# Out-projection of an attention block by seven quarter products per pair of heads, on normalised probabilities

## The chip, the cores and the metric

The kernel runs on one core of a Trainium2 chip. The metric is the device time of one execution in microseconds; the median of three runs before the change is 1045.25 us (1043.97 to 1045.48). Times of single instructions come from one profiled execution.

The engines are TensorE (PE; its weight loads are listed as PEld), VectorE (DVE), ScalarE (ACT), GpSimd (POOL) and SyncE (SP), which here only issues DMAs. Each works through its own instructions in order. [...]

## What is computed

The reference is a transformer block with adaptive LayerNorm, all in fp32: batch 2, 1024 tokens, width 256, 16 heads of 128.

```python
h = layernorm(x) * (1 + ca) + sa
q, k, v = h @ Wq + bq, h @ Wk + bk, h @ Wv + bv      # 16 heads of 128; rotary on q and k
attn = softmax(causal(q @ k.T * 128 ** -0.5))        # per head, 1024 x 1024
x = x + ga * ((attn @ v) joined over heads @ Wo + bo)
h = layernorm(x) * (1 + cb) + sb
x = x + gb * down(silu(gate(h)) * up(h))             # 704 hidden, int32 weights with scales
```

`sa, ca, ga, sb, cb, gb` come from a small product of `silu(c)` with `wmod`.

## The kernel before

Tokens lie on 128 partitions in 8 tiles (`NT`) or, turned, in two halves of 512 columns (`NB` blocks). The unit of work is one head of one batch: 32 units, `units[n] = (b, g, h)`, two heads `h` to a pair `g`, eight pairs to a batch. Everything sits in one hand-written order, `with tc.manual_schedule()` (L1008): what the program emits is the order of each engine's queue, and there is no planner.

The main loop (L1064) runs over units and within a unit over eight rows `i`, one per tile of 128 queries. A row does this:

- `shared_out` (L1004) emits one tile of the out-projection of an earlier unit, 13 rows behind.
- `score` (L601): TensorE computes `ps`, 128 queries against (i + 1) x 128 keys, into one of two score buffers; one DVE instruction adds the mask in place and gives the negated row maximum `nmax`.
- `turned` (L643) of the row before: DVE turns 32 x 32 blocks of the probabilities into `t32`; after each fourth row SP issues 16 DMAs that move the blocks across partitions into `pT` (one block of queries). `t32` has four slots of equal size for the four rows of a block.
- `expo` (L628): ACT computes the exponential of the row and, in the same pass, its sum `dens`.
- `set_step` (L464): the products of q, k and v of the coming units. From the second pair on, a 1024 x 256 by 256 x 256 projection is already made of seven products of quarters with sums of quarters, with adds on DVE, ACT and POOL and sums of weights on POOL (`weight_sums`).
- rotary embedding (`rotary_sums`, L583): two ACT copies and three POOL operations for each half of q or k, at rows set by `TURNS`.
- `values` (L663): `po` = v-transposed times `pT`, for the unit before: block 0 in row 0 (four matmuls), block 1 in rows 6 and 7 (eight). One PSUM bank holds `po`; ACT copies it to `outs`.
- `extras` (L912): the weight fold, LayerNorm pieces of the next stage, weight loads of the FFN, and the like.

The probabilities are not normalised. `project_out` (L708) multiplies a tile of `outs` with the head's part of Wo (128 x 256) into the single bank `py`, and one DVE instruction adds it to x, times the reciprocal of the row sum:

```python
nc.vector.scalar_tensor_tensor(
    x[b][:, t, :], py[:, :D], rdens[u][:, t : t + 1], x[b][:, t, :], ALU.mult, ALU.add
)
```

So each pair has 16 such matmuls of 256 columns, each with weights of its own (a tile of `outs`), and 16 updates of x. `fold_out` (L382) multiplies Wo with the gate `ga` on POOL, in row 2 of a pair's first unit, and for batch 0 it also gathers what the bias of v gives through Wo. `bias_row` (L397) turns that into a row with one matmul in unit 16, and `add_bias` (L406) adds it to x by 16 POOL operations.

The last unit runs the first products of the FFN of batch 0 in its rows. After the loop come the rest of the FFN products, the out-projection tiles still owed, and the FFN of batch 1.

Of the kernel before, what the change touches and what calls it, by code (L numbers as in the profile page):

```python
# [37 lines left out]
def adaln_block(ctx: ExitStack, tc: tile.TileContext, a, cos_d, sin_d, out):  # L38
# [74 lines left out]
    bvacc = const.tile([P, D], F32, name="bvacc")  # L113
# [100 lines left out]
    opool = pool("attnT", 2)  # L214
# [99 lines left out]
    def ffn_weight_load(n):  # L314
        if n == "gate":
            t = fpool.tile([P, KC * 2 * HID], I32, tag="f", name="raw")
            at = 0
            for m, w in (("gate", FULL), ("up", FULL), ("last", P)):
                raws[m] = t[:, at : at + KC * w].rearrange("p (k h) -> p k h", k=KC)
                at += KC * w  # L320
        nc.scalar.dma_start(raws[n], a[f"wq_{n}"])
# [6 lines left out]
    def ffn_down_load():  # L328

        for c, (pool_, tag, bufs) in (  # L330
# [3 lines left out]
            nc.scalar.dma_start(t, a["wq_down"][:, c : c + 2, :])  # L334
        sbc["down"] = small.tile([P, D], F32, tag="bw", bufs=1, name="s_down")
        nc.scalar.dma_start(sbc["down"], a["scales"][:, 2 * HID :].to_broadcast([P, D]))
# [38 lines left out]
    def load_out(b, g):  # L375
        t = wpool.tile([P, HG, D], F32, tag="wo", name=f"wo_{b}{g}")
        nc.sync.dma_start(
            t, a["L0_attn_Wo"][g]
        )
        weights[b, g]["o"] = t  # L380

    def fold_out(b, g):  # L382
        t = weights[b, g]["o"]
        if b == 0:

            for h in range(HG):
                c = R_BV + g * HG + h
                bw = small.tile([P, D], F32, tag="bw", bufs=1, name=f"bw_{g}{h}")
                nc.gpsimd.tensor_scalar(bw, t[:, h, :], cols[:, c : c + 1], None, ALU.mult)
                nc.gpsimd.tensor_tensor(bvacc, bvacc, bw, ALU.add)  # L390

        for h in range(HG):
            nc.gpsimd.tensor_tensor(t[:, h, :], t[:, h, :], gate["a", b], ALU.mult)

    gbo = {}

    def bias_row():  # L397

        pb = ps_a.tile([P, 512], F32, tag="a", name="pbias")
        nc.tensor.matmul(pb[:, :D], ones, bvacc, start=True, stop=True)  # L400
        nc.vector.tensor_tensor(bo_bc, pb[:, :D], bo_bc, ALU.add)
        gbo.update({0: bvacc, 1: bo_bc})
        for b in range(B):
            nc.gpsimd.tensor_tensor(gbo[b], gate["a", b], bo_bc, ALU.mult)

    def add_bias(b, t):  # L406
        nc.gpsimd.tensor_tensor(x[b][:, t, :], x[b][:, t, :], gbo[b], ALU.add)

    vs, qks, outs, dens, rdens, probs, pTs = {}, {}, {}, {}, {}, {}, {}
    weights = {}  # L410
# [230 lines left out]
    t32 = [const.tile([P, 4, 4, 4 * (j + 1), 32], F32, name=f"t32_{j}") for j in range(NB)]  # L641

    def turned(u, i):  # L643
# [4 lines left out]
            t32[blk][:, :, j, : i + 1, :].rearrange("p c k b -> p k c b"),  # L648
            p[:, : (i + 1) * P].rearrange("p (k c a) -> p k c a", c=4, a=32),
        )  # L650
        if j < 3:
            return
        pT = ptpool.tile(
            [P, 4, 4, 4 * (blk + 1), 32], F32, tag=f"pT{blk}", name=f"pT_{b}{g}{h}{blk}"
# [8 lines left out]
    def values(u, blk, k0, k1):  # L663
        b, g, h = u
        if blk == 0 and k0 == 0:
            outs[u] = opool.tile([P, S], F32, tag="o", name=f"o_{b}{g}{h}")
        if k0 == 0:
            pos[u, blk] = ps_o.tile([P, 512], F32, tag="o", name=f"po_{b}{g}{h}{blk}")
        po = pos[u, blk]
        last = 4 * blk + 3  # L670
        pT = pTs[u, blk].rearrange("p r i k b -> p i r k b")
        for k in range(k0, k1):
# [4 lines left out]
                pT[:, off:, :, k, :],  # L677
# [3 lines left out]
        if k1 == last + 1:  # L681
            nc.scalar.copy(outs[u][:, ts(blk, QB)], po)  # L682
# [25 lines left out]
    def project_out(u, t, late=False):  # L708

        b, g, h = u  # L710
        if t % 4 == 0:
            nc.vector.reciprocal(rdens[u][:, t : t + 4], dens[u][:, t : t + 4])
        name = f"py_{b}{g}{h}{t}"
        py = lane(name) if late else ps_y.tile([P, 512], F32, tag="y", name=name)
        nc.tensor.matmul(  # L715
# [196 lines left out]
    def extras(n, i):  # L912

        if i == (2 if n else 7) and units[n][2] == 0:
            fold_out(*units[n][:2])
# [336 lines left out]
```

## Time and profile before

| | |
|---|---|
| median of the runs | 1045.25 us |
| profiled execution | 1044.49 us |
| its span on the core | 1042.7 us |
| instructions | 13636 |
| granted TensorE clock | 1.00 |
| DMA traffic | 131.86 MB, mean 126 GB/s |
| scores (L613) / values (L674) / out-projection (L715), share of the chain that ended last | 22% / 23% / 10% |

The page gives for each engine its busy time and share of the span. A line of the groups names the source line, engine, operation, tiles written and read, shape and count; then the busy time of the group and the mean duration of one in ns; then the engine's idle time just before them with what ended it. A line of the timeline begins with start and duration in us, and ends, in brackets, with the idle time before it and its releaser. An fp32 matmul is recorded as two MATMUL instructions, and a record includes the time in which the last columns leave the array, so that neighbours overlap. A few matmul records can be missing.

### The profile page before, as it was taken

How to read it: one execution, taken by the hardware profiler on the slowest of the kernel's cores; microseconds unless marked ns; L12 is line 12 of the kernel's file. 1: busy time of each engine (PE TensorE's matmuls, PEld its weight loads, DVE VectorE, ACT ScalarE, POOL GpSimd, SP SyncE). 2: the span in 40 equal slices, each digit the busy share in tenths (PEclk: the TensorE clock that was granted, in tenths of full speed). 3: DMA queues.
4: the chain of work that ended last, by engine and by line, in shares of the span. 5: the costliest groups of instructions: out<-in, count | busy, mean ns of one | idle time of the engine just before them, and what ended most of it. 6: DMA issues, size and time to landing. Idle time of an engine off the chain costs nothing.

```text
span 1042.7 us, 13636 instructions
## 1 busy us (share of the span) xinstructions
PE 1029.0 (99%) x3766; PEld 623.5 (60%) x3766; DVE 759.5 (73%) x1619; ACT 506.3 (49%) x997; POOL 745.6 (72%) x768
## 2 busy tenths in 40 slices
PE   9999999999999999999999999999999999999998
PEld 5655565656556565656565666656565656555737
DVE  5667877787777777767776767677878866787573
ACT  5654545555545445455555554554635545353230
POOL 4738787979787878998787878787876778831131
PEclk9999999999999999999999999999999999999999
DMA  5365555665554545665555545454555557532101
GB/s 193 82 180 137 150 131 144 165 162 147 132 138 103 137 120 143 154 152 124 124 145 122 134 116 144 111 141 110 148 131 128 141 138 176 130 76 62 45 1 41
DMA packets 67616, 131.86 MB, mean 126 GB/s; under 512 B 19110, under 2 KB 22708, under 8 KB 67540
## 3 DMA queue, kind: packets, MB, share of 16 engines
q1 hardware_dynamic: 65292, 125.65, 49.1%
q10 hardware_dynamic: 2168, 5.20, 1.5%
q8 instruction: 31, 0.51, 0.2%
q14 instruction: 45, 0.37, 0.1%
q0 software_dynamic: 80, 0.13, 0.1%
HBM read 25.52 MB, written 2.10 MB: 26 GB/s over the span
## 4 chain that ended last, share of the span: by engine, by line
PE 89%; DVE 6%; POOL 2%; DMA 1%; issue 1%; ACT 1%; SPq 0%; DVEq 0%; POOLq 0%; ACTq 0%
PE po L674 23%; PE ps L613 22%; PE py L715 10%; PE pv L489 8%; PE pq L493 8%; PE pk L493 7%; PE pgu L766 4%; PE pd L878 2%; PE pq L552 1%; PE pk L552 1%; PE pv L420 1%; PE pd_0w L878 1%; PE pd_1w L878 1%; DVE x L718 1%; DMA cols<-in_biases 1%
## 5 line engine op out<-in xcount | busy, mean ns | idle before, releaser
L633 ACT ACTIVATE p<-ps,nmax 128x128 f32<-128x128 f32 (+7 forms) x256 | 189.7, 741 | 356.3 <-DVE nmax L616 347.7
L613 PE MATMUL ps<-kT,qT 128*128 128x512 f32 (+3 forms) x768 | 289.9, 486 | 1.0 <-POOL kT L592 1.0
L674 PE MATMUL po<-pT,v 128*128 128x512 f32 (+3 forms) x768 | 263.4, 486 | 0.0
L616 DVE CUSTOM_DVE_ANT_0 ps<-ps,mask 128x128 f32<-128x128 f32 (+7 forms) x256 | 195.1, 762 | 77.9 <-PE ps L613 75.8
L674 PEld LDWEIGHTS po<-pT,v 128*128 128x128 f32 x768 | 144.7, 190 | 134.2 <-issue 106.2
L718 DVE SCALAR_TENSOR_TENSOR x<-py,rden,x 128x256 f32<-128x256 f32 x255 | 121.5, 478 | 133.0 <-PE py L715 128.7
L647 DVE STREAM_TRANSPOSE t<-p 128x128 f32<-128x128 f32 (+7 forms) x256 | 198.2, 774 | 7.6 <-ACT p L633 3.6
L613 PEld LDWEIGHTS ps<-kT,qT 128*128 128x128 f32 x768 | 145.7, 190 | 78.8 <-issue 63.6
L715 PE MATMUL py<-wo,o 128*128 128x256 f32 x510 | 153.0, 384 | 6.2 <-DVE x L718 6.2
L715 PEld LDWEIGHTS py<-wo,o 128*128 128x128 f32 x510 | 87.7, 191 | 80.1 <-issue 49.7
L590 POOL TENSOR_TENSOR r_k<-r_k,sin_t 128x512 f32<-128x512 f32 x56 | 71.3, 1273 | 84.6 <-ACT r_k L589 84.5
L590 POOL TENSOR_TENSOR r_q<-r_q,sin_t 128x512 f32<-128x512 f32 x56 | 71.9, 1285 | 27.5 <-ACT r_q L589 25.3
L589 ACT COPY r_q<-qT 64x512 f32<-64x512 f32 x112 | 69.1, 617 | 29.0 <-POOL qT L500 27.3
L592 POOL TENSOR_TENSOR kT<-kT,r_k 128x512 f32<-128x512 f32 x56 | 71.2, 1271 | 4.4
L592 POOL TENSOR_TENSOR qT<-qT,r_q 128x512 f32<-128x512 f32 x56 | 71.0, 1267 | 4.4
L591 POOL TENSOR_TENSOR qT<-qT,cos_t 128x512 f32<-128x512 f32 x56 | 71.3, 1273 | 0.0
L591 POOL TENSOR_TENSOR kT<-kT,cos_t 128x512 f32<-128x512 f32 x56 | 71.2, 1272 | 0.0
L589 ACT COPY r_k<-kT 64x512 f32<-64x512 f32 x112 | 69.1, 617 | 2.2 <-DVE kT L500 0.2
L682 ACT COPY o<-po 128x512 f32<-128x512 f32 x64 | 37.5, 586 | 43.6 <-PE po L674 43.4
L489 PEld LDWEIGHTS pv<-wv,tT 128*128 128x128 f32 x336 | 44.1, 192 | 17.1 <-issue 11.2
L774 POOL TENSOR_TENSOR gsnap<-gsnap,gsnap 128x512 f32<-128x512 f32 x8 | 10.5, 1308 | 56.2 <-DVE gsnap L774 56.2
L633 ACT ACTIVATION_READ_ACCUMULATOR p<-ps,nmax 128x1 f32 x256 | 49.4, 193 | 0.0
(222 smaller groups left out, 1495.4 us busy)
## 6 DMA issues: line engine op xcount, KB each, us to landing
pT<-t SPq DMA_DIRECT2D x512, 128.0 KB, 2.4
pT<-t SPq DMA_DIRECT2D x512, 64.0 KB, 2.0
wq<-in_Wq SPq DMA_DIRECT2D x16, 256.0 KB, 3.1
wk<-in_Wk SPq DMA_DIRECT2D x16, 256.0 KB, 2.9
wv<-in_Wv SPq DMA_DIRECT2D x16, 256.0 KB, 2.8
wo<-in_Wo SPq DMA_DIRECT2D x16, 256.0 KB, 2.9
out<-x SPq DMA_DIRECT2D x15, 128.0 KB, 1.7
x<-in_x ACTq DMA_DIRECT2D x4, 256.0 KB, 3.9
```

The lines of the kernel that those rows point to most:

```text
L493: nc.tensor.matmul(bank, wq, tokens, start=True, stop=True)
L589: nc.scalar.copy(r1[to], q[of])
L590: nc.gpsimd.tensor_tensor(r1, r1, sin_t[:, sl], ALU.mult)
L591: nc.gpsimd.tensor_tensor(q, q, cos_t[:, sl], ALU.mult)
L592: nc.gpsimd.tensor_tensor(q, q, r1, ALU.add)
L613: nc.tensor.matmul(ps[:, c:e], qT[:, ts(i, P)], kT[:, c:e], start=True, stop=True)
L616: nc.vector.tensor_tensor_reduce(ps[:, :L], ps[:, :L], mask[:, NT - 1 - i :, :].rearrange("p t k -> p (t k)"), -SCALE, FLT_MAX, ALU.add, A ...
L633: nc.scalar.activation(p[:, :L], ps[:, :L], AF.Exp, bias=nmax, scale=-1.0, accum_out=dens[u][:, i : i + 1])
L647: nc.vector.transpose(t32[blk][:, :, j, : i + 1, :].rearrange("p c k b -> p k c b"), p[:, : (i + 1) * P].rearrange("p (k c a) -> p k c a", ...
L674: nc.tensor.matmul(po[:, off * P :], vs[b, g][:, k, ts(h, DH)], pT[:, off:, :, k, :], start=(k == 0), stop=(k == last),)
L715: nc.tensor.matmul(py[:, :D], outs[u][:, ts(t, P)], weights[b, g]["o"][:, h, :], start=True, stop=True)
L718: nc.vector.scalar_tensor_tensor(x[b][:, t, :], py[:, :D], rdens[u][:, t : t + 1], x[b][:, t, :], ALU.mult, ALU.add)
```

## The change

For each pair of heads but the last one of batch 1 (`direct`), the out-projection is done by seven quarter products in place of sixteen tile products. The 1024 tokens are halved (`blk`), the pair's 256 rows of Wo are halved by head, and the 256 output columns are halved. `out_product` makes one product of 512 tokens by 128 columns, four matmuls of 128 x 128; left factors are quarters of `outs` or their sums (`out_sum`, four DVE operations per pair), right factors are quarters of Wo or their differences (four POOL operations per pair in `fold_out`). Three products go straight to x (one of them subtracted), four are gathered over the pairs of a batch in `m1`, `m5`, `m6`, `m7`, and after the batch's last pair `out_total` brings those to x by eight operations. `OUTS`, `SUMS` and `TOTALS` give the rows: a pair's products lie in rows 2, 6 and 7 of the second unit after its first head, and 0, 2, 4 and 6 of the next.

Sums over two heads need normalised heads. So each row has, after its exponential, a reciprocal of its one column of `dens` on DVE (`inverse`) and a pass of ACT over the row's probabilities with that column as scale (`divided`), before the turn. The bias of v is added where ACT evacuates `po`; the gathered bias products, the bias matmul and the additions to x go, and `bias_row` now puts the gated output bias into `m1` and `m5`.

The turned probabilities are packed: row j of a block starts at slot `STEP * j`, so that `t32` and `pT` have 13 and 29 slots in place of 16 and 32. `outs` has single buffers per half and head, and memory freed or needed elsewhere moves: the FFN weights are loaded in place, two chunks of the FFN's activations share the `m` buffers. The fold of Wo moves to row 6 of a pair's first unit. The load of the down weights moves from ACT's queue at unit 29, row 7, to SP's queue at unit 30, row 5. The load of Wo comes after that of Wk. At unit 16 the turns of rows 0 and 1 change places. In the last unit row 5 has no FFN products; after the loop come 3 tile products instead of 2 (or 3) in each group, and 7 FFN products instead of 5 in the last call. The totals of batch 1 fall into rows 3 to 7 of the last unit, in part on POOL.

```diff
     def fold_out(b, g):
         t = weights[b, g]["o"]
-        if b == 0:
-            for h in range(HG):
-                c = R_BV + g * HG + h
-                bw = small.tile([P, D], F32, tag="bw", bufs=1, name=f"bw_{g}{h}")
-                nc.gpsimd.tensor_scalar(bw, t[:, h, :], cols[:, c : c + 1], None, ALU.mult)
-                nc.gpsimd.tensor_tensor(bvacc, bvacc, bw, ALU.add)
         for h in range(HG):
             nc.gpsimd.tensor_tensor(t[:, h, :], t[:, h, :], gate["a", b], ALU.mult)
+        if (b, g) == direct:
+            return
+        b11, b12, b21, b22, t1, t2, t4 = wquarters[b, g]
+        for to, x0, x1 in ((t1, b12, b11), (t2, b22, t1), (b12, b22, b12), (t4, t2, b21)):
+            nc.gpsimd.tensor_tensor(to, x0, x1, ALU.subtract)
...
+    STEP = [4 * blk + 3 for blk in range(NB)]
+    SLOTS = [3 * STEP[blk] + 4 * (blk + 1) for blk in range(NB)]
+    def inverse(u, i):
+        nc.vector.reciprocal(rdens[u][:, i : i + 1], dens[u][:, i : i + 1])
+    def divided(u, i):
+        p = probs[u, i][:, : (i + 1) * P]
+        nc.scalar.activation(p, p, AF.Copy, scale=rdens[u][:, i : i + 1])
...
         if k1 == last + 1:
-            nc.scalar.copy(outs[u][:, ts(blk, QB)], po)
+            c = R_BV + g * HG + h
+            nc.scalar.activation(outs[u, blk], po, AF.Identity, bias=cols[:, c : c + 1])
...
+    def out_sum(b, g, n):
+        h0, h1 = ((b, g, h) for h in range(HG))
+        if n == 3:
+            osum[3] = opool.tile([P, QB], F32, tag="oC", name=f"o3_{b}{g}")
+            nc.vector.tensor_tensor(osum[3], outs[h0, 1], outs[h0, 0], ALU.subtract)
+        elif n == 1:
+            osum[1] = outs[h0, 0]
+            nc.vector.tensor_tensor(osum[1], osum[1], outs[h1, 0], ALU.add)
+        elif n == 2:
+            osum[2] = outs[h0, 1]
+            nc.vector.tensor_tensor(osum[2], osum[1], osum[2], ALU.subtract)
+        else:
+            osum[4] = opool.tile([P, QB], F32, tag="oC", name=f"o4_{b}{g}")
+            nc.vector.tensor_tensor(osum[4], outs[h1, 1], osum[2], ALU.subtract)
...
+    def out_product(b, g, n):
...
+        py = ps_y.tile([P, 512], F32, tag="y", name=f"py_{b}{g}_{n}")
+        for j in range(QB // P):
+            nc.tensor.matmul(py[:, ts(j, P)], left[:, ts(j, P)], right, start=True, stop=True)
+        flat, py = py, by_tiles(py)
+        if n in (2, 3, 4):
+            blk, half = {2: (1, 0), 3: (1, 1), 4: (0, 0)}[n]
+            to = quarter_of(b, blk, half)
+            nc.vector.tensor_tensor(to, to, py, ALU.subtract if n == 4 else ALU.add)
+            return
+        if g:
+            to = by_tiles(total[b, n])
+            nc.vector.tensor_tensor(to, py, to, ALU.add)
+            return
...
+    OUTS = {2: (1,), 6: (4,), 7: (7,), 8: (5,), 10: (6,), 12: (2,), 14: (3,)}
+    SUMS = {6: (3, 1, 2), 8: (4,)}
+    TOTALS = {6: (0,), 11: (1,), 13: (2, 3), 14: (4, 5), 15: (6, 7)}
...
             for i in range(NT):
-                shared_out(8 * n + i - 13)
+                out_steps(n, i, False)
+                last = (u, i - 1) if i else (prev, NT - 1)
                 ps, nmax = score(u, i)
-                if i >= 1:
-                    turned(u, i - 1)
-                elif prev:
-                    turned(prev, NT - 1)
+                if last[0]:
+                    turned(*last)
                 expo(u, i, ps, nmax)
                 release()
...
+                inverse(u, i)
+                divided(u, i)
+                out_steps(n, i, True)
...
-                at = TURNS[h].get(i)
+                at = TURNS[h].get(1 - i if n == 16 and i < 2 else i)
...
-                    gate_ups(0, 2, late=False)
+                    gate_ups(0, 0 if i == 5 else 2, late=False)
...
-            for _ in range(2 + (c == 3)):
+            for _ in range(3):
                 shared_out(s, late=True)
...
-        gate_ups(0, 5)
+        gate_ups(0, 7)
```

## The prediction

> **What bounds the kernel now.** I read four views in this order: the busy table of the page, the groups of instructions split by shape, the stretches unit by unit, and the timeline of one unit's end.
>
> ```profile
> PE 1029.0 (99%) x3766; PEld 623.5 (60%) x3766; DVE 759.5 (73%) x1619; ACT 506.3 (49%) x997; POOL 745.6 (72%) x768
> ```
>
> TensorE is busy for 99%. A matmul's record has a pipelined tail, so the next view shows whether it is really full.
>
> ```profile
> 557.18:584.71 27.53, 27.53 (x85) 15.33 (x84) 20.14 (x42) 15.63 (x32) 23.00 (x22) 1.00 0.58 144
> 584.82:613.35 28.53, 28.53 (x129) 19.20 (x128) 20.22 (x42) 13.00 (x28) 22.48 (x26) 1.00 0.51 121
> 753.74:783.79 30.05, 29.16 (x129) 19.30 (x128) 23.14 (x51) 13.06 (x28) 21.26 (x24) 1.00 0.48 115
> ```
>
> Columns: stretch, length, then busy time of PE, weight loads, DVE, ACT, POOL, and the granted clock. The first two stretches are the second and first head of a quiet pair: PE fills both, DVE needs 20 us of 28. The third also carries the next LayerNorm: it is 1.5 us longer, and PE is idle in it.
>
> ```profile
> L715 PE MATMUL py<-wo,o 128*128 128x256 f32 x510 | 153.0, 384 | 6.2 <-DVE x L718 6.2
> L489 PE MATMUL pv<-wv,hT 128*128 128x128 f32 x336 | 44.3, 275 | 0.0
> ...
> L718 DVE SCALAR_TENSOR_TENSOR x<-py,rden,x 128x256 f32<-128x256 f32 x255 | 121.5, 478 | 133.0 <-PE py L715 128.7
> ...
> L633 ACT ACTIVATE p<-ps,nmax 128x1024 f32<-128x1024 f32 x32 | 35.7, 1115 | 141.4 <-DVE nmax L616 141.4
> ...
> L589 ACT COPY r_k<-kT 64x512 f32<-64x512 f32 x112 | 69.1, 617 | 2.2 <-DVE kT L500 0.2
> ...
> L509 ACT ACTIVATE snapk<-pk,cols 128x512 f32<-128x512 f32 x14 | 9.5, 680 | 0.6 <-PE pk L493 0.6
> ```
>
> An fp32 matmul is two records. A record's mean holds the tail, so I price TensorE by the distance between starts:
>
> ```profile
> 522.94 0.59 PE L715 MATMUL py<-wo,o 128*128 128x256 f32 x2
> 523.37 1.88 PE L613 MATMUL ps<-kT,qT 128*128 128x512 f32 x4
> 525.29 1.23 DVE L616 CUSTOM_DVE_ANT_0 ps<-ps,mask 128x1024 f32<-128x1024 f32 x1 [1.23 <-PE ps L613]
> 526.67 1.11 ACT L633 ACTIVATE p<-ps,nmax 128x1024 f32<-128x1024 f32 x1 [3.89 <-DVE nmax L616]
> ...
> 483.88 1.06 PE L489 MATMUL pv<-wsv,tT 128*128 128x128 f32 x8
> 484.77 0.59 PE L493 MATMUL pk<-hT,wk 128*128 128x512 f32 x1
> ```
>
> One 256-column matmul takes 523.37 - 522.94 = 0.43 us (0.432 is the usual distance), four of 128 columns take 484.77 - 483.88 = 0.89, or 0.222 each; 512 columns take 0.858. By these a pair of heads holds 56.1 us of TensorE work. Starts of the first score of each pair lie 56.2 apart in quiet stretches (557.18, 613.35). From 99.37 to 896.40, 14 pairs, the excess over 56.17 is 10.6 us: 1.2 is a score that waited for kT at 482, 0.4 the bias matmul, and about 9 is TensorE waiting for DVE to free the single py bank, mostly in the LayerNorm units.
>
> **The change part by part.** All against the profiled execution, 1044.5 us (span 1042.7); the median of the runs is 0.8 above it.
>
> Products. A pair's 16 matmuls of 256 columns (16 x 0.432 = 6.91) become 28 of 128 columns (28 x 0.222 = 6.22): 0.69 us less. Fifteen of sixteen pairs: **-10.3**. They lie on the path, as PE is. The bias matmul goes: **-0.4**.
>
> [...] The trace has 0.111 us for a 128-column pass and 0.216 for one of 256, so price follows width. [...]
>
> DVE. Out go 255 updates of x (121.5) and 64 reciprocals (9.8). In come 256 one-column reciprocals at 0.15 (38; the row of 128x4 has 154 ns), 60 sums of 128x512 at 0.71 to 0.78 (45; rows of sums from SBUF), 101 adds from PSUM at 0.67 (68), 12 totals (9), 16 direct updates at 0.42 (7): 167 for 131, so DVE goes to about 796, 76%. The wait is what matters: the reciprocal of row i stands in DVE's queue behind the exponential of row i, and ahead of the next row's maximum. Behind it wait the sums, the next add and that maximum, and ACT's division.
>
> ACT. 256 divisions, SBUF to SBUF with a scale column, are not in the trace. From below: silu from SBUF, 128x512, 0.628; from above: the copy from SBUF, 0.617, plus 0.10, what the column operand adds between a copy (0.58) and L509 (0.68) from PSUM. With the exponential's slope of 0.107 per 128 columns, 1024 columns cost 1.05 to 1.14. I take 1.10, 0.73 in the mean, 187 us. With 64 evacuations at 0.68 instead of 0.586 ACT goes to about 700, 67%.
>
> POOL loses 40 us (bias products, row additions) and gains 60 x 0.455 + 7.5 = 35. The weight fold moves from row 2 to row 6 of a pair's first unit, 3.3 us in one piece: queued behind it is only the last k rotation, wanted at row 4 of the next unit, some 10 us later. [...]
>
> Queues. SP issues as many turns as before, each with 19% or 9% fewer bytes: hidden, 10 us of issuing as now (16 x 0.63). The output weights' load swaps places with wk (0.5 us later, wanted 20 us later). The down weights' four loads leave ACT's queue for SP's, at row 5 of unit 30 instead of row 7 of unit 29; wanted in row 1 of unit 31, they still have about 8 us. The turn swapped at unit 16 should remove the kT wait: **-1**, its bounds 0 and -1.2.
>
> Unit's end, from when the last score row has streamed (525.09 = 523.37 + 4 x 0.43). DVE: maximum at 0.20, transpose at 1.35, an add at 2.38, reciprocal 2.96 to 3.11. ACT: exponential from 1.58 to 2.69, so the reciprocal waits for nothing. Division from 3.2 to 4.25-4.34; only then the evacuation of po, which now stands behind it (at 3.2 before): 0.68, to 4.9-5.0. TensorE wants that bank at 5.0 (v product 0.89, po 2.16, product 5 0.89, score 0.22, q product 0.86; after the second head also 5.0) and needs 0.16 to restart. The stall is 0 to 0.15 a unit; I take 0.07, **+2** over 31 units. A gain is excluded, as nothing waited there.
>
> Rows 1 to 5 of a first head. DVE's loop a row is maximum + 0.155 + exponential + 0.3: with the one py add 9.5 us for the five rows. TensorE has 10.5. The hops fit by a microsecond, and two score banks let TensorE run ahead. In the six LayerNorm units 3 us come on top, where one py add now stands for five updates of 0.4. I expect the 9 us of waits to fall to 5: **-4**, bounds -9 and +6.
>
> Last unit. DVE gets four adds of products, a sum and three totals for eight updates of x, beside the FFN's work: about 30 us against 28 of TensorE: **+2.5**, bounds 0 and +5. The tail has 16 direct products at the end where 13 were; they only change places with products of the FFN.
>
> Sum: -10.3 - 0.4 - 1 + 2 - 4 + 2.5 = -11.2, so 1033.3 for a profiled execution and **1034.0** for the median.
>
> **Rivals.**
>
> The unit's end decides. The division is dearer than bounded, or DVE reaches the last maximum late, and po waits 0.6 us at each of 31 starts: 18.6 instead of 2, **1051**. For: ACT's evacuation lost a cover of 1.1 us, the margin is zero. Against: row 6 holds 7 us of TensorE work in which DVE catches up. It turns the sign at 0.42 us.
>
> The row loop decides. If each of its hops is 0.4 us longer than the rows say, five rows of 15 first heads overshoot by 1.0: **+15**, 1049. For: 347.7 us that ACT waited for maxima show how tightly they are coupled. Against: DVE's 9.5 against 10.5.
>
> All waits vanish. One py bank turns seven times a pair instead of sixteen, so the 9 us go, the unit's end costs nothing, nor does the last unit: 1034 - 5 - 2 - 2.5 = **1024.5**.
>
> Gains and waits cancel: 1041 to 1049, half of each rival.
>
> **How the numbers follow.** Forecast, 1029 to 1041: 0.46. All waits vanish, below 1029: 0.15. Cancel: 0.14, of it 0.05 faster, 0.07 the same, 0.02 slower. Unit's end: 0.12. Row loop: 0.13. A measurement can tell 0.2%, about 2 us, from no change: faster 0.66, same 0.07, slower 0.27. The range 1023 to 1053 leaves out the better part of the best case and of both slow ones, under 0.2.
>
> **What would show it.** Right: the groups of 128x128 py with 840 records at 0.275 us mean; quiet pairs 55.5 us apart; the evacuation of po ending within 0.2 us of TensorE's need; DVE near 796, ACT near 700. Wrong: PE's waits naming ACT's evacuation at each unit's first po, or scores waiting for the exponential two rows back; a 1024-column division above 1.3 us; product 7 waiting for its sum in row 7.

## The result and the profile after

The changed kernel takes 1078.89 us (median; 1077.23 to 1079.94) against 1044.72 us for the kernel before (1043.97 to 1045.48): a ratio of 1.0326, 95% interval 1.0308 to 1.0344. It is 34 us slower where 11 us faster was forecast, and outside the predicted range. The profiled execution's span is 1078.2 us, before 1042.7.

The busy table of the changed kernel; below it the shares by engine of the chain of work that ended last, first of the changed kernel, then of the kernel before:

```profile
PE 1036.7 (96%) x4124; PEld 623.2 (58%) x4124; DVE 839.1 (78%) x1743; ACT 697.6 (65%) x1257; POOL 767.6 (71%) x783
...
PE 39%; DVE 25%; ACT 12%; POOL 8%; SPq 8%; issue 5%; DMA 2%; DVEq 0%; ACTq 0%; POOLq 0%
...
PE 89%; DVE 6%; POOL 2%; DMA 1%; issue 1%; ACT 1%; SPq 0%; DVEq 0%; POOLq 0%; ACTq 0%
```

ScalarE came out as computed (700), VectorE 43 us above (796), GpSimd 27 us above (741). TensorE is 96% "busy", yet only 39% of the chain lies on it where 89% did: most of the rest is work of VectorE (25%) and ScalarE (12%) that TensorE waits for. A record's busy time includes its tail (a record of 512 columns lasts 0.59 us, and the next starts 0.429 us after it began), so TensorE's losses are better read from the distances between the starts of matmuls. What is over the streaming time (0.111, 0.216, 0.323 and 0.429 us a record of 128, 256, 384 and 512 columns) in distances that are over it by more than 60 ns adds up to about 21 us before and 66 us after.

The stretches that answer to those of the prediction, in the changed kernel (length, then busy time of PE, weight loads, DVE, ACT, POOL; clock; DMA share). The first two make up a quiet pair, second head of one pair and first head of the next; the third also carries LayerNorm:

```profile
574.20:601.93 27.73, 27.25 (x94) 14.81 (x93) 20.34 (x44) 21.41 (x40) 21.77 (x22) 1.00 0.52 129
601.93:630.72 28.79, 28.79 (x147) 19.68 (x146) 24.21 (x48) 18.85 (x35) 24.50 (x27) 1.00 0.45 106
775.75:805.59 29.84, 29.36 (x147) 19.68 (x145) 26.30 (x57) 18.93 (x35) 25.60 (x28) 1.00 0.44 102
```

The pair takes 56.5 us, and each of the two quiet pairs after it 57.6, where 55.5 was expected. The clock is full in these stretches. Elsewhere it is not: in the changed kernel the granted clock stands at 0.50 twice, for 3.41 us each, from 91.7 and from 962.1 us; this is the first time, with the 3.4 us ahead of it, in which TensorE is busy for only 1.28 us (columns as above):

```profile
88.26:91.68 3.42, 1.28 (x3) 0.68 (x4) 2.81 (x6) 1.20 (x2) 1.19 (x1) 1.00 0.34 85
91.68:95.09 3.41, 3.41 (x5) 1.35 (x4) 3.41 (x7) 2.33 (x5) 2.41 (x3) 0.50 0.32 80
```

Records of 512 columns start 0.85 us apart there instead of 0.43, so such a stretch costs about 1.7 us, half of its length, on top of the wait. The kernel before has none. Of the 16 profiled executions 9 have one or two, 15 in all, and each time TensorE had waited 1.7 to 2.9 us at one place within the few us before; but waits of that length without such a stretch occur too (2.3 us at 88 us in the run with the later k rotation). Where it bears on a comparison it is named below.

What became dearer is in the groups by shape:

```profile
L756 PE MATMUL py<-wo,o 128*128 128x128 f32 x840 | 111.7, 276 | 4.2 <-DVE o L724 4.2
...
L638 ACT ACTIVATE p<-p,rden 128x1024 f32<-128x1024 f32 x32 | 36.7, 1148 | 13.8 <-DVE rden L634 13.8
...
L727 DVE TENSOR_TENSOR o<-o,o 128x512 f32<-128x512 f32 x15 | 24.6, 1642 | 0.5
L730 DVE TENSOR_TENSOR o<-o,o 128x512 f32<-128x512 f32 x15 | 24.6, 1639 | 0.5
...
L724 DVE TENSOR_TENSOR o<-o,o 128x512 f32<-128x512 f32 x15 | 20.4, 1357 | 0.0
...
L733 DVE TENSOR_TENSOR o<-o,o 128x512 f32<-128x512 f32 x15 | 18.3, 1222 | 0.0
```

The products (276 ns) are what the prediction took, and the division (1.148 us for 1024 columns) lies 0.05 above its price. The 60 sums of outputs are not: 87.9 us for 45, a sum 1.22 to 1.64 us where 0.71 to 0.78 was taken. The timeline of a first head's rows 6 and 7, and of the start of the second head at 574.20, shows why (start, duration, then the instruction; in brackets idle time before it and what ended it):

```profile
565.61 1.28 POOL L579 TENSOR_TENSOR qT<-qT,cos_t 128x512 f32<-128x512 f32 x1
...
565.71 1.72 DVE L724 TENSOR_TENSOR o<-o,o 128x512 f32<-128x512 f32 x1
...
566.96 1.59 POOL L580 TENSOR_TENSOR qT<-qT,r_q 128x512 f32<-128x512 f32 x1
567.46 1.64 DVE L727 TENSOR_TENSOR o<-o,o 128x512 f32<-128x512 f32 x1
...
567.57 1.13 PE L756 MATMUL py<-wo,o 128*128 128x128 f32 x8 [0.96 <-DVE o L724]
...
568.51 1.72 POOL L488 TENSOR_TENSOR v<-snapv,snapv 128x512 f32<-128x512 f32 x1
...
569.13 1.64 DVE L730 TENSOR_TENSOR o<-o,o 128x512 f32<-128x512 f32 x1
...
570.70 1.22 DVE L604 CUSTOM_DVE_ANT_0 ps<-ps,mask 128x1024 f32<-128x1024 f32 x1
...
573.45 0.14 DVE L634 RECIPROCAL rden<-den 128x1 f32<-128x1 f32 x1
573.62 1.15 ACT L638 ACTIVATE p<-p,rden 128x1024 f32<-128x1024 f32 x1 [0.40 <-DVE rden L634]
...
574.67 0.67 ACT L680 ACTIVATE o<-po,cols 128x512 f32<-128x512 f32 x1
...
575.37 1.25 ACT L577 COPY r_k<-kT 64x512 f32<-64x512 f32 x2
...
576.69 1.27 POOL L578 TENSOR_TENSOR r_k<-r_k,sin_t 128x512 f32<-128x512 f32 x1 [1.90 <-ACT r_k L577]
...
577.92 1.72 POOL L579 TENSOR_TENSOR kT<-kT,cos_t 128x512 f32<-128x512 f32 x1
...
579.72 1.27 POOL L580 TENSOR_TENSOR kT<-kT,r_k 128x512 f32<-128x512 f32 x1
...
580.95 0.46 POOL L443 TENSOR_TENSOR wq<-wq 128x128 f32<-128x128 f32 x1
...
581.49 0.46 POOL L444 TENSOR_TENSOR wq<-wq 128x128 f32<-128x128 f32 x1
...
581.99 1.12 PE L481 MATMUL pq<-tT,wq 128*128 128x512 f32 x2 [0.48 <-POOL wq L444]
```

Sum and GpSimd instruction take turns in these rows. The sum at 565.71 ends 0.54 us after the rotation that was in flight (565.61 + 1.28 = 566.89), and the rotation that starts at 566.96 lasts 1.59 instead of 1.27. The next sum waits for that one (568.55) and ends at 569.10, and so on: three sums take 5.1 us where 2.1 to 2.3 were reckoned. In 59 of the 60 sums the duration is the rest of the GpSimd instruction in flight plus 0.535 to 0.581 us; the sixtieth, which met one only in its last 7 ns, took 0.662.

From there two things spread. Product 7 (567.57) comes 1.1 us late by the distance of starts, as its sum (L724) is the first of the three. And the k rotation, whose copies stand on ScalarE behind the division and the evacuation (575.37), holds up what is queued behind it on GpSimd: the sums of Wq come at 580.95 and 581.49, and the q product of the next unit waits for them. In the table of waits of the changed kernel (engine, line and what ended the wait: us in total, times, longest):

```profile
ACT p L638 <- DVE rden L634: 96.2, 186, 4.0
...
DVE rden L634 <- ACT p L621: 66.2, 93, 5.0
...
PEld po L671 <- ACT o L680: 31.7, 30, 2.5
...
PEld pq L481 <- POOL wq L444: 13.3, 12, 1.2
```

ScalarE waits 96 us for reciprocals, and VectorE 66 us for the exponentials that these need: each row passes twice more from engine to engine. These two figures are not a loss by themselves: the run with the later k rotation, below, has 98.0 and 54.0 us of them, and quiet pairs of 55.5. What counts is where TensorE waits. By distances between matmuls, up to the first record of the product that waited, the changed kernel loses 12.8 us in waits for the evacuation of po, 7.9 for the Wq sums, 5.8 for the sum of product 7 and 3.8 for the value evacuation in the LayerNorm units. (The second record of such a product comes another 0.10 us late; with it the first two are 14.5 and 9.1.) The 8.6 us that the kernel before lost to its single py bank are gone.

### The profile page after: what moved, and what is told of

The parts are those of the page before. It is cut to its first block, busy times and chain, and to the rows that moved or that the text cites. A ratio compares the mean times of both kernels' runs of the same rounds, so it can differ in the third digit from the quotient of the medians.

```text
span 1078.2 us, 14476 instructions
## 1 busy us (share of the span) xinstructions
PE 1036.7 (96%) x4124; PEld 623.2 (58%) x4124; DVE 839.1 (78%) x1743; ACT 697.6 (65%) x1257; POOL 767.6 (71%) x783
## 4 chain that ended last, share of the span: by engine, by line
PE 39%; DVE 25%; ACT 12%; POOL 8%; SPq 8%; issue 5%; DMA 2%; DVEq 0%; ACTq 0%; POOLq 0%
PE po L671 9%; PE ps L601 8%; SPq L656 6%; PE pq L481 4%; DVE ps L604 4%; DVE t L644 3%; PE pgu L839 3%; PE pk L481 3%; ACT p L638 3%; ACT p L621 3%; ACT r_k L577 2%; PE py L756 2%; PE pv L477 2%; DVE o L727 2%; DVE o L730 2%
## 5 line engine op out<-in xcount | busy, mean ns | idle before, releaser
L671 PE MATMUL po<-pT,v 128*128 128x512 f32 (+3 forms) x768 | 268.7, 493 | 10.1 <-ACT o L680 10.1
L638 ACT ACTIVATE p<-p,rden 128x128 f32<-128x128 f32 (+7 forms) x256 | 198.6, 776 | 96.3 <-DVE rden L634 96.2
L644 DVE STREAM_TRANSPOSE t<-p 128x128 f32<-128x128 f32 (+7 forms) x256 | 198.0, 773 | 20.7 <-ACT p L638 12.8
L601 PEld LDWEIGHTS ps<-kT,qT 128*128 128x128 f32 x768 | 133.0, 191 | 103.1 <-issue 95.6
L756 PEld LDWEIGHTS py<-wo,o 128*128 128x128 f32 x840 | 105.9, 192 | 37.0 <-issue 31.5
L756 PE MATMUL py<-wo,o 128*128 128x128 f32 x840 | 111.7, 276 | 4.2 <-DVE o L724 4.2
L634 DVE RECIPROCAL rden<-den 128x1 f32<-128x1 f32 x256 | 39.0, 152 | 66.3 <-ACT p L621 66.2
L580 POOL TENSOR_TENSOR qT<-qT,r_q 128x512 f32<-128x512 f32 x56 | 75.9, 1356 | 4.4
L579 POOL TENSOR_TENSOR kT<-kT,cos_t 128x512 f32<-128x512 f32 x56 | 77.7, 1388 | 0.0
L481 PE MATMUL pq<-tT,wq 128*128 128x512 f32 x84 | 44.4, 610 | 7.4 <-POOL wq L444 5.9
L481 PE MATMUL pk<-hT,wk 128*128 128x512 f32 x84 | 44.4, 610 | 6.1 <-ACT snapv L503 2.8
```

The source lines that it names most:

```text
L481: nc.tensor.matmul(bank, wq, tokens, start=True, stop=True)
L579: nc.gpsimd.tensor_tensor(q, q, cos_t[:, sl], ALU.mult)
L580: nc.gpsimd.tensor_tensor(q, q, r1, ALU.add)
L601: nc.tensor.matmul(ps[:, c:e], qT[:, ts(i, P)], kT[:, c:e], start=True, stop=True)
L638: nc.scalar.activation(p, p, AF.Copy, scale=rdens[u][:, i : i + 1])
L644: nc.vector.transpose(t32[blk][:, :, STEP[blk] * j :, :][:, :, : i + 1, :].rearrange("p c k b -> p k c b"), p[:, : (i + 1) * P].rearrange( ...
```

## The experiments

For each run the three stretches of its profiled execution stand in one table: from the start to the first score of unit 3, from there to unit 31 (14 pairs), and from unit 31 to the end. The time is the ratio to the kernel before. A star marks a stretch of half clock in a profiled execution, about 1.7 us each.

| kernel | ratio [95%] | start | middle | end |
|---|---|---|---|---|
| before | 1 | 99.4 | 797.0 | 146.3 |
| changed | 1.0326 [1.0308, 1.0344] | 103.0* | 817.2 | 157.9* |
| fold back in row 2 | 1.0298 [1.0283, 1.0313] | 101.8 | 814.5 | 158.0* |
| no sums | 1.0074 [1.0059, 1.0089] | 100.6 | 796.1 | 154.1 |
| no division | 1.0005 [0.9994, 1.0017] | 101.3 | 790.3 | 151.6 |
| neither | 0.9936 [0.9913, 0.9960] | 101.4* | 786.1 | 151.3 |
| sums of one input | 1.0162 [1.0139, 1.0184] | 103.1* | 802.2 | 155.5* |
| sums spread | 1.0139 [1.0124, 1.0154] | 100.1 | 802.4 | 154.6 |
| sums spread, k turn later | 1.0077 [1.0056, 1.0099] | 101.1 | 796.0 | 154.3 |
| the same, sums on GpSimd | 1.0160 [1.0133, 1.0186] | 100.3 | 804.0* | 156.3* |
| changed, evacuation first | 1.0285 [1.0258, 1.0312] | 102.6* | 815.7 | 154.5* |
| spread, later, evacuation first | 1.0095 [1.0070, 1.0121] | 102.8* | 798.4 | 154.6* |
| before, with the division | 1.0201 [1.0176, 1.0227] | 103.1 | 815.2** | 148.1 |
| before, with packed turns | 0.9992 [0.9981, 1.0004] | 99.3 | 797.7 | 146.3 |
| spread, later, no late totals | 1.0053 [1.0036, 1.0070] | 101.7 | 797.6 | 154.2* |
| spread, later, unit 31 undivided | 1.0049 [1.0033, 1.0065] | 101.5 | 797.5 | 151.3 |

### The fold back in row 2

```diff
-        if n % 2 == 0 and n != 14 and i == 6 or (n, i) == (14, 3):
+        if n % 2 == 0 and i == (2 if n else 6):
```

> The changed kernel with the fold of Wo back in row 2 of a pair's first unit (row 6 of unit 0). Theory F: in row 6 the fold's 3.3 us on POOL stand ahead of the sums of Wq, and product 3 of q waits for these in row 2 of the second unit (9.2 us in 12 units of the trace). F expects these waits gone and 8 to 10 us less, about 1070. If the sums of outs on DVE (theory P) or the division on ACT (theory D) hold the units up, other waits take the place and the time stays within 3 us of 1079.

Measured: 1076.23 us, ratio 1.0298. TensorE still waits 7.8 us for the Wq sums (7.9 in the changed kernel). The fold is not what holds them; by the rows at 575 to 582 it is the k rotation that stands ahead of them, which a later run tests. The 3 us that the run gains lie at the edge of the intervals; its profiled execution has one stretch of half clock where that of the changed kernel has two, which may be 1.7 of them.

### Without the sums

```diff
     def out_sum(b, g, n):
         h0, h1 = ((b, g, h) for h in range(HG))
+        osum[n] = {1: outs[h0, 0], 2: outs[h0, 1], 3: outs[h0, 0], 4: outs.get((h1, 1))}[n]
+        return
```

> The changed kernel without the sums of outs on DVE: four instructions per pair are left out, and products 3, 5, 6 and 7 take plain quarters of outs, so the out-projection computed is another one. Theory P: these 60 sums take 88 us instead of 45, three of them form a block of 5 us in row 6, and so product 7 (5.9 us of waits) and the last maximum of the unit, hence the division and the evacuation of po (18 us of waits), come late. P expects 20 to 24 us less, 1055 to 1059. Theory D (the division on ACT alone makes the evacuation late) expects only the 6 us of product 7, about 1073.

Measured: 1052.56 us, ratio 1.0074. VectorE falls from 839.1 to 754.8, 84.3 us for 60 sums, or 1.4 each. GpSimd falls too, from 767.6 to 741.1, though none of its instructions went: the sums had cost it 26.5 us, 0.44 each. Quiet pairs take 55.8 to 55.9 us, and the waits on the Wq sums fall to 2.3.

### Without the division

```diff
     def divided(u, i):
+        return
```

> The changed kernel without the division on ACT: 256 instructions, 199 us of ACT, are left out, the reciprocals stay, and the probabilities go on unnormalised, so the output is another one. Theory D expects the evacuation of po to be free (18 us) and the rows' loop shorter: 1055 or less, with product 7's waits and the waits for the sums of Wq left. Theory P alone, in which DVE's block in row 6 is the hold-up, expects less than 8 us from it, since DVE's work is the same: 1071 or more.

Measured: 1045.36 us, ratio 1.0005, quiet pairs 55.5 to 55.7. The sums are nearly as slow as before, 81.7 us in all for 87.9; the two slowest groups:

```profile
L728 DVE TENSOR_TENSOR o<-o,o 128x512 f32<-128x512 f32 x15 | 24.6, 1641 | 0.5
...
L731 DVE TENSOR_TENSOR o<-o,o 128x512 f32<-128x512 f32 x15 | 23.3, 1553 | 0.5
```

(These are L727 and L730 of the changed kernel, one line lower.) So slow sums cost far less where the division is left out.

### Without both

Both edits above.

> Leaves out the 60 sums of outputs and the 256 divisions of probabilities (the products take an unsummed output, the probabilities stay undivided, so the output differs). If the saving of the products is as large as the prediction has it, and sums and division hold all the rest, the quiet pairs stay at 55.5 us and the waits on the Wq sums go: 1034 to 1040, the excess over 1034 in the last unit. If the products themselves cost more than their distances say, it stays at 1044 or above, as either one left out alone gave (1045.4, 1052.6).

Measured: 1039.9 us, ratio 0.9936, just within the upper end expected. With this the two causes can be set apart, in us of the kernel before (1 per mille is 1.04): neither -6.7, sums alone +0.5, division alone +7.7, both +34.1. The sums by themselves cost 7, the division by itself 14, and together they cost 41: nearly half of the loss comes only when both are there. (The intervals are some 2 us wide on either side. The stretches of half clock are in these figures, some 2 to 3 us of the +34.1 and none of the +7.7.) The 256 reciprocals of one column, and the other moves of the change, are in all four versions and were not taken apart.

The middle of this run is what the prediction computed for the products. Its 14 pairs take 10.9 us less than before; 14 x 0.69 + 0.4 + 1 = 11.1 was reckoned. The streaming time by the distances of starts falls by 10.2 us in them. TensorE's waits hardly fall, from 11.6 to 10.2 us: the 8.3 for the py bank and the 1.2 for kT are gone, and 8.0 have come, for evacuations and additions of q, k and v. The 4 us that the prediction expected from the py bank are therefore not there even without sums and division. The two ends, in which the start holds 1.7 us of half clock, were not foreseen either and are taken up last.

### Sums of one input

```diff
-            nc.vector.tensor_tensor(osum[3], outs[h0, 1], outs[h0, 0], ALU.subtract)
+            nc.vector.tensor_scalar(osum[3], outs[h0, 1], 1.0, None, ALU.mult)
```

and the same for the other three.

> Each of the 60 sums becomes an operation of the same shape, in the same place, that reads one of its two inputs and multiplies it by 1.0 (the second input is left out, so the output differs). If a VectorE operation with two SBUF inputs must wait for the GpSimd instruction in flight, and one with a single input needn't, the four groups fall from 1.22 to 1.64 us to below 0.7 us and the time to within 3 us of the run without sums (1052 to 1056). If any VectorE operation between SBUF tiles waits so, they stay above 1.2 us and the time above 1070.

Measured: 1062.69 us, ratio 1.0162: between the two expectations, and the reading that a sum waits for GpSimd only because it has two inputs falls: with one it still takes 1.04 to 1.49 us, by groups, where that reading expects less than 0.7. The groups:

```profile
L727 DVE TENSOR_SCALAR o<-o 128x512 f32<-128x512 f32 x15 | 22.3, 1489 | 0.0
...
L730 DVE TENSOR_SCALAR o<-o 128x512 f32<-128x512 f32 x15 | 20.6, 1372 | 0.5
...
L724 DVE TENSOR_SCALAR o<-o 128x512 f32<-128x512 f32 x15 | 17.6, 1173 | 0.0
L733 DVE TENSOR_SCALAR o<-o 128x512 f32<-128x512 f32 x15 | 15.7, 1044 | 0.0
```

A scaling from SBUF to SBUF waits in the same way: its duration is the rest of the GpSimd instruction in flight plus 0.281 to 0.319 us. What is left after that instruction is about half of what a sum has left (medians 0.285 and 0.547). GpSimd loses 9 us to these operations (750.5 for 741.1) where it lost 26.5 to the sums. But "any operation between SBUF tiles" is wrong as well: in the same trace the 32x32 transposes of 128x1024, from SBUF to SBUF, take 1.233 to 1.246 us with a GpSimd instruction in flight and 1.241 without, and additions with one operand in PSUM, where TensorE left it (qT<-pq,snapq), 0.65 either way.

### Sums spread

```diff
-    SUMS = {6: (3, 1, 2), 8: (4,)}
+    SUMS = {0: (3,), 6: (1,), 7: (2,), 8: (4,)}
```

> The changed kernel with the same sums in other rows: the one for product 7 in row 0, where DVE has 2 us to spare, the one for product 5 in row 6, the one for product 6 in row 7. Theory P expects the block in row 6 to fall from 5.0 to 1.7 us, product 7's waits to vanish and most of the waits at the unit's end with them: 12 to 18 us less, 1061 to 1067. Theory D expects only product 7's 6 us. If the sums just push what follows them wherever they stand, nothing is won.

Measured: 1059.32 us, ratio 1.0139. The same 60 sums, one to a row, give back 19.6 us. Product 7 no longer waits, nor does TensorE at the ends of the quiet units; the 8 us of waits for the Wq sums remain.

### The k rotation behind the Wq sums

The spread sums, and

```diff
-        {0: ("q", 1, 0), 1: ("k", 0, 1), 3: ("k", 1, 0), 5: ("q", 1, 1), 7: ("k", 1, 1)},
+        {0: ("q", 1, 0), 1: ("k", 0, 1), 3: ("k", 1, 0), 5: ("q", 1, 1)},
```

so that the last k rotation falls to row 0 of the next unit, where the second table has it.

> The sums spread as in the spread run (one each in rows 0, 6, 7, 0), and the last k rotation (head 1, second half) begins in row 0 of the next unit instead of row 7, so that the Wq sums stand ahead of it on GpSimd. If the q product waits because the sums stand behind a rotation whose copies come late on ScalarE, its 8.0 us of waits fall below 2 and the time to 1050 to 1053. If the rotation is then late for the score row that needs it, a wait of TensorE for kT takes its place and the time stays at 1058 or above.

Measured: 1053.96 us, ratio 1.0077. The waits for the Wq sums are gone, and no wait for kT took their place: the chain was rotation, then Wq sums, then q product, and the stall is the rotation's. The quiet pair that answers to the one shown of the changed kernel:

```profile
559.68:586.45 26.77, 26.77 (x95) 14.91 (x94) 19.64 (x44) 21.20 (x40) 21.03 (x22) 1.00 0.52 124
586.45:615.23 28.78, 28.78 (x147) 19.76 (x145) 22.49 (x48) 19.66 (x36) 25.44 (x29) 1.00 0.47 114
```

A quiet pair now takes 55.5 to 55.6 us with all of its sums and divisions in it, the length that the prediction had. What the middle still loses against the run without both (796.0 for 786.1) lies in seven of the 14 pairs, those with LayerNorm among them: they take 57.5 to 60.6 us here and 56.6 to 57.5 there.

### The same, with the sums on GpSimd

```diff
-            nc.vector.tensor_tensor(osum[3], outs[h0, 1], outs[h0, 0], ALU.subtract)
+            nc.gpsimd.tensor_tensor(osum[3], outs[h0, 1], outs[h0, 0], ALU.subtract)
```

and the same for the other three.

> As the run with spread sums and the later k rotation (1054), with the 60 sums issued by GpSimd instead of VectorE. They can then not hold up VectorE: its busy time falls from 806 to about 762 us, GpSimd's rises from 761 to about 835 (1.27 us a sum). If what that version still loses in the middle (796 us against 786 without sums and divisions) is VectorE's time, 1047 to 1052. If GpSimd's own order (rotations, Wq sums) is the tighter one, its later sums make the q product or the k rotation late: above 1056.

Measured: 1062.35 us, ratio 1.0160, 8.7 us worse by the ratios than on VectorE; its profiled execution has two stretches of half clock, 3.4 us, the other none. A sum takes GpSimd 1.27 us, and VectorE is down to 760.3. Quiet pairs stay at 55.5 to 55.6; the loss is in the others and in the last unit. In the table of waits TensorE waits for a sum of GpSimd, and longer than before for the q evacuation of VectorE (7.7 in the run before it):

```profile
PEld pk L481 <- DVE snapq L488: 10.0, 7, 3.1
...
PEld py L756 <- POOL o L727: 3.5, 3, 2.9
```

The second expectation holds in time and in the wait for the sums; why the q evacuation comes later was not followed. Spread sums on GpSimd are dearer here than spread sums on VectorE.

### The evacuation ahead of the division

```diff
                 inverse(u, i)
-                divided(u, i)
+                if i < 7 or not prev:
+                    divided(u, i)
...
                 if i in (6, 7) and prev:
                     values(prev, 1, 4 * (i - 6), 4 * (i - 5))
+                    if i == 7:
+                        divided(u, i)
```

> The changed kernel with one order turned: in row 7 the evacuation of po stands ahead of the division on ScalarE instead of behind it. If the unit's end is lost there, TensorE's waits for that evacuation (about 14 us by distances between matmuls) fall below 4 and the time to 1065 to 1070; the waits for product 7 (5.9) and for the Wq sums (9.2) stay. If the division is what the rest hangs on, it comes 0.7 us later, the next unit's rows with it, and the time stays above 1074.

Measured: 1075.54 us, ratio 1.0285. The waits for the evacuation went, as the first theory has it, and the time did not:

```profile
PEld pq L481 <- POOL wq L444: 17.4, 12, 2.1
...
PE pq L481 <- POOL wq L444: 10.1, 12, 1.5
...
PEld pk L481 <- ACT snapv L503: 6.9, 8, 1.2
...
PEld ps L601 <- ACT p L621: 6.0, 14, 1.0
```

Waits for the Wq sums, the value evacuation and the exponential took their place (by distances the Wq sums' rose from 7.9 to 12.0 us). So the stall on po was where the lateness came out, not where it was made. The same turn on the spread version:

> The run with spread sums and the later k rotation (1054), with the same turned order in row 7. Its waits for the evacuation were already near 2 us, so little is left to gain: 1051 to 1054. Above 1056 would say that the division is needed at once.

Measured: 1055.65 us, ratio 1.0095. There was nothing left to gain there; whether the turn costs anything, the intervals don't tell.

### The division alone, and the packing alone, on the kernel before

```diff
+                inverse(u, i)
+                divided(u, i)
...
-        nc.vector.scalar_tensor_tensor(
-            x[b][:, t, :], py[:, :D], rdens[u][:, t : t + 1], x[b][:, t, :], ALU.mult, ALU.add
-        )
+        nc.vector.tensor_tensor(x[b][:, t, :], py[:, :D], x[b][:, t, :], ALU.add)
```

> The kernel before, with only the normalisation moved: a reciprocal and a division by ScalarE in each row, and a plain addition in place of the scaled update of x. If the division alone makes the unit's end late, as in the run without sums (quiet pairs 55.9 instead of 55.5, and Wq waits), 1050 to 1060, with TensorE's waits naming the evacuation of po and the q product. If it is harmless until a late sum stands ahead of it, 1045 to 1048.

Measured: 1068.27 us, ratio 1.0201, above both expectations. The division needs no late sum to do harm: on the kernel before it costs 21 us, more than the 14 beside the new products. Three of its four executions, the profiled one among them, have stretches of half clock; the fourth has none and takes 1064.26, so some 4 of the 21 us are these. There 16 products a pair wait for the one py bank, and VectorE, which now waits for an exponential in many rows (69.6 us), frees it later: TensorE's waits for the update of x make 13.2 us by distances (8.6 before), two of them of 2.1 us, each followed by half clock. The waits for the evacuation of po make 3.5 and those for the Wq sums 2.7, and quiet pairs take 56.8 to 57.0.

The packed turns by themselves:

```diff
-    t32 = [const.tile([P, 4, 4, 4 * (j + 1), 32], F32, name=f"t32_{j}") for j in range(NB)]
+    STEP = [4 * blk + 3 for blk in range(NB)]
+    SLOTS = [3 * STEP[blk] + 4 * (blk + 1) for blk in range(NB)]
+    t32 = [const.tile([P, 4, SLOTS[blk], 32], F32, name=f"t32_{blk}") for blk in range(NB)]
```

> The kernel before with one part of the change alone: the turned probabilities packed (19% or 9% fewer bytes in the turns). If the turns were hidden on both sides, no difference: 1043 to 1047. If fewer bytes shorten a path, below 1042.

Measured: 1044.43 us, ratio 0.9992 [0.9981, 1.0004]: no difference, as priced.

### The last unit

Both on the version with spread sums and later k rotation. Without the late totals:

```diff
-                for step in TOTALS.get(at, ()) if last else ():
+                for step in TOTALS.get(at, ()) if last and not b else ():
```

> As the run with spread sums and the later k rotation (1054; its stretch from unit 31 to the end 154.3 us), with the second batch's eight totals left out (its output lacks the totals). If the totals are what the last unit lost, the stretch falls to 150 or below and the time to 1050 or below. If they are hidden, it stays at 153.5 to 155.

Measured: 1051.46 us, ratio 1.0053; the stretch from unit 31 stays at 154.2. By the expectation this would say that they are hidden. But this execution has a stretch of half clock after the start of unit 31 (first row below), which costs 1.7 us, and the run that it is compared with has none. And a wait of that run (second row: TensorE waits for an exponential, 1.7 us by distance) is gone without the totals (third row, the same products in this run):

```profile
915.26:918.67 3.41, 3.36 (x9) 2.32 (x10) 2.73 (x5) 1.08 (x3) 3.17 (x7) 0.50 0.00 0
...
935.60 1.10 PE L839 MATMUL pgu<-tT,wupT 128*128 128x512 f32 x2 [1.56 <-ACT p L621]
...
937.74 1.10 PE L839 MATMUL pgu<-tT,wupT 128*128 128x512 f32 x2
```

So the totals are not hidden: they cost about 1.7 us, as the stretch would take 152.5 at full clock, between the two expectations. The times agree with that (2.5 us less, though the intervals overlap). How the totals delay the exponential was not followed.

```diff
-                divided(u, i)
+                if nxt:
+                    divided(u, i)
```

> As the same run, with the eight divisions of unit 31 left out (its probabilities stay undivided, so the output differs). If ScalarE is late there because of them, TensorE's waits for the exponential and for the evacuation in unit 31 go (1.7 and 0.9 us) and the stretch from unit 31 falls to 150 to 152. If the wait before unit 31, or the GpSimd work that comes late into it, is the cause, it stays above 153.

Measured: 1050.77 us, ratio 1.0049; the stretch falls to 151.3, the length that it has without any sum or division. So 3.0 of that version's 8.0 us are the division of unit 31. Of the 5.0 that are left 0.9 is work: 3 products of 0.89 and 16 direct ones of 0.432 come after the first score of unit 31, where 20 of 0.432 did. The wait for the exponential is down to 0.84 us in this run, so division and totals share it, and it is open how much of the 4.1 that are left would go with the totals. The distances also show TensorE waiting 0.85 and 1.91 us early in unit 31 for FFN weight sums and token sums of GpSimd (0.70 in the kernel before), and 1.04 for an update of x.

## Why the prediction was wrong

**Products, bias, kT: right.** The middle of the run without sums and divisions is 10.9 us shorter, for 11.1 reckoned, and 10.2 of it are streaming time. The price of a 128-column pass from the distance of starts held (840 records at 276 ns, quiet pairs at 55.7 in that run). The kT wait of 1.16 us, still there with the packed turns alone, is gone in the changed kernel.

**"60 sums of 128x512 at 0.71 to 0.78 (45; rows of sums from SBUF)": the first step that failed.** They took 87.9. All of VectorE's excess over 796 is this term. The price taken is near that of a sum that meets no GpSimd instruction (0.67 in the spread runs); the trace of before already held the other case. In the kernel before, the scaling of LayerNorm, SBUF to SBUF, lists its spread (minimum, median, maximum in ns):

```profile
L246 DVE TENSOR_SCALAR xn_a<-x,mv_a,rstd_a x16: 406/414/1272, 7.3 to 367.3; 128x256 f32<-128x256 f32 x16
L246 DVE TENSOR_SCALAR xn_b<-x,mv_b,rstd_b x16: 408/414/1277, 760.7 to 970.7; 128x256 f32<-128x256 f32 x16
```

Of those 32 the 21 that met no GpSimd instruction took 0.41, the other 11 0.48 to 1.28. The price has no time in which VectorE waits for GpSimd; in the changed kernel GpSimd lost 0.44 us a sum, and VectorE about 0.7 (1.46 in the mean for 0.71 to 0.78).

**"The stall is 0 to 0.15 a unit; I take 0.07, +2": the step that decides.** It was computed from a last row in which VectorE comes on time. Row 6 was to give VectorE the time to catch up; instead it holds the 5.1 us of sums. In the changed kernel the evacuation of po costs 12.8 us by distances, near the 18.6 of the rival "the unit's end decides", but not as that rival has it: 9.7 of it come at the starts of second heads alone, after a row 6 with three sums, mostly 0.7 us each time, and the whole falls to 2.7 when the sums are left out or spread. Two of the prediction's signs of being wrong thus came: this wait, if only at every other unit, and product 7 waiting for its sum. Nor is the place the cause: the order on ScalarE turned, the wait went and the time fell by only 3 us. The failure lies in pricing the division by its last hop. It puts a crossing from VectorE to ScalarE into the chain of maximum, exponential, reciprocal and division of every row; taken out of the changed kernel it is worth 34 us, and with the sums gone 14. That the chain has no slack left is inferred from this and from the spread sums, which with the division in place give back 19.6 us. The loss came out at product 7, at po and at the q product, and moved from one to the other when one was relieved.

**"queued behind it is only the last k rotation": wrong in the queue, not in the fold.** Behind that rotation on GpSimd stand the sums of Wq, with a q product waiting. It is late because its copies stand on ScalarE behind the new division. Moving the fold changed nothing in this; moving the rotation took the waits away, and 6 us of the time.

**ScalarE, GpSimd's own work, queues: right, ScalarE's total in part by luck.** The divisions are 0.776 us in the mean for 0.73, 198.6 us for 187; ScalarE still comes out at 697.6 for 700 because busy time counts overlapping records once, and 52 us of them overlap now where 36 did. The price of a division is not what failed. GpSimd's total is 741.1 without the sums for 740.6, and the packed turns cost and gain nothing.

**"I expect the 9 us of waits to fall to 5": wrong.** The py waits went altogether, but waits for evacuations of v on ScalarE and of q on VectorE replace them, mostly in the same units: 8.3 us by distances in the version with spread sums and later rotation, and about as much already without sums and division. This term of -4 was thus worth about nothing.

**"Last unit +2.5": wrong, and the start was left out.** The last stretch grew by 11.6, of it 0.9 moved work and 1.6 half clock; the first by 3.6, though 1.6 us of products had moved out of it (4 quarter products of 0.89 before unit 3 for 12 of 0.432). In the first stretch TensorE waits 2.6 us at 88 us for a qT of VectorE where it had waited 0.1, then 1.7 us go to half clock; earlier, at 47 us, it waits 0.7 us for the value evacuation on ScalarE. Why that qT comes late was not followed; it does so in every version but the packed turns.

The sum therefore runs: -11.2 predicted; -6.7 measured without sums and division, the ends and the waits that did not fall making the difference; +7 for the slow sums; +14 for the division; +19 for the two together; +34 measured. No version that does the whole change beat the kernel before; the nearest is 0.8% slower.

## What to carry to other kernels

Before pricing a VectorE sum or scaling that only touches SBUF, look at what GpSimd runs at that moment: here the rest of its instruction came on top (1.22 to 1.64 us a sum, by groups, where one that met none took 0.67), and three in a row took 5.1 us for the 2.1 to 2.3 reckoned. Spread such sums (one to a row was worth 19.6 us here), or put them where GpSimd is idle; do not stack them ahead of a chain that must be on time. And price an operation that is inserted into a loop between engines by the loop, not by the one hop where its engine has room: a stall that vanishes when its place is relieved, with the time unchanged, was only where the lateness came out.

## What the runs showed of the hardware

In the changed kernel 59 of the 60 VectorE sums of two SBUF tiles (128x512, fp32) ended 0.535 to 0.581 us (median 0.547) after the end of the GpSimd instruction that was in flight when they began; in the run with scalings of one SBUF tile in their place it was 0.281 to 0.319 (median 0.285). The 47 GpSimd additions or products of 128x512 that began during a sum of the changed kernel lasted 1.6 to 1.7 us instead of 1.27. Transposes of 32x32 blocks (1.23 to 1.25 us at 128x1024), and additions with an operand in PSUM (0.65), lasted the same with a GpSimd instruction in flight and without.

In 9 of the 16 profiled executions the granted clock stood at 0.5 for 3.41 us, 15 times in all, each time within a few us after TensorE had waited 1.7 to 2.9 us at one place. In the changed kernel records of 512 columns started 0.85 us apart in it instead of 0.43, so that the late operand cost its wait and about 1.7 us more. Not every such wait was followed by it (2.3 us at 88 us in the run with the later k rotation), and no run shows what decides.
